# A fused conditioning and attention kernel: division on two engines, first sequences in rows, later weight loads

## The chip, the cores and the metric

The kernel runs on one core of one Trainium2 chip. That core has a tensor engine (PE), a vector engine (DVE), a scalar engine (ACT), GpSimd (POOL) and a sync engine (SP); SP and ACT also issue DMAs. The metric is the device time of one execution in microseconds (us); lower is better. All data are fp32, and weights and inputs start in the chip's memory.

## The reference

There are 32 sequences (B) of 256 tokens (S) with 256 features (D). For each, a cross attention with 16 heads of 16 conditions the input, a transformer of two layers follows (8 heads of 64, a window of 128 tokens with look-back, and a gated feed-forward part with 682 hidden units), and the input is added:

```python
# cond: seq1 = x (keys, values), seq2 = f (queries), seq_len1 = lengths
q = ((seq2 + b_self) @ Wq + bq);  k = (concat([seq1 + b_prev, seq2 + b_self], 1) @ Wk + bk)
v = (concat([seq1, seq2], 1) @ Wv + bv)                  # each split in 16 heads
score_prev = where(arange(l1) < seq_len1, q @ k[:l1].T * SCALE, -inf)
score_self = (q * k[l1:]).sum(-1, keepdims=True) * SCALE   # each query's own token
w = softmax(concat([score_prev, score_self], -1))
cond = (w[..., :-1] @ v[:l1] + w[..., -1:] * v[l1:]) @ Wo + bo
# each of two layers, on h (shift_token: half of the features one token later)
q, k, v = split(shift_token(h) @ wqkv, 3)
q, k = rotary_xpos(l2norm(q) * qs, l2norm(k) * ksc)
h = h + local_attention(q, k, v) @ wo                   # softmax over own and previous window
n = layernorm(shift_token(h)) * lg + lb
a, g = split(n @ w1 + b1, 2);  h = h + (a * gelu(g)) @ w2 + b2
out = x + h
```

## The kernel before

**The planner.** The kernel is not written in the order in which it runs. `tile_kernel` calls methods of `Engine` objects, which only record operations into a `Plan`. PE's operations are recorded in units (`plan.unit`), each with a kind of tiling of the array: full, split in rows (2 or 4) or in columns (2 or 4). `price` gives each operation a cost. `run` then walks the five engines in time by these costs: PE takes the unit with the best `score`, another engine the ready operation with the lowest `rank`. `score` takes the age of a unit (a due time from `PERIOD`, its place, and offsets from the lists `SHIFT`, `FIRST` for the first group and `FINAL` for the last two), a price for another tiling, the backlog that the unit would add to an engine (`STAY`, `ENTER`), and the PSUM banks that it takes (`BANKS`). A full unit marked soft may be cut into column parts when PE is in a column tiling (`parted`). At the end `issue` emits everything in that order, so nearly every instruction of the profile has one line, L567, and is told by its tile's name. A tile written by `either` goes to DVE or ACT, as the planner finds.

**Setup, stage (-1, 0).** `load_sequence(0)` and `load_sequence(1)` load f and x of the first two sequences with `blocks`: four DMAs of 64 KB per tensor on SP, in runs of 128 bytes, so that 32x32 blocks lie as DVE's transpose wants them. ACT's queue carries `wq`, `wk`, `wv`, the biases, `misc` (with the identity and the masks), `wo`, the rope table `rope0`, and in a loop over both layers 15 DMAs each: `wqkv`, the scales, `wout`, `w1`, the norm's vectors, `b1`, `w2`. Each layer has a `b1` unit on PE: its bias plus `w1` applied to the norm's offset `lb`, 40 records of one column and 4 for a packed remainder.

**A group.** There are 16 groups of two sequences (G = 2), in the loop over p:

- `prepared`: DVE transposes f and x into `fT` and `xT` (STREAM_TRANSPOSE). PE projects `cq`, `ck`, `cs` and `vals`; ACT adds biases into `qc` and `kc`. `spread` copies them by 8 DMAs each on SP into `qh` and `kh`, where each head has 16 of 32 rows, and 4 more bring the length mask (`behind`) into `kh`. `self` gives each token's score with itself.
- `conditioned`: four units of scores `S` in row tiling, whose maxima DVE reduces into `mx`; `nm`; a turn `nmT`; `rows` on ACT, and four DMAs of it into `qh`. Then the scores again, transposed (`ST`), exponentials `eT` on ACT, `AV` in column tiling, `oh`, the turn `ohT`, the quotient `at` on POOL, `turn` and the projection `co` into the residual stream `res`.
- `attention`, per layer and sequence: `q`, `k` and `v`; squares `sq` on ACT, their sums `ss`, the rotary products `raw` and `rot` on DVE and POOL; turns `qkT`; scores `sc`; in `weights` the masked maximum, the exponential with its sum `den`, its reciprocal and the division of `ex`; turns `exT`, copied on ACT; `av`; `wout`.
- `feedforward`, per layer for both sequences: the mean, `cen`, `var`, `rstd`, its turn `rs`, `w1` with the gate, `w2`.
- `finished`: DVE turns the result back (`yt`), POOL adds the input, four DMAs store it.

The division of `weights` in this version, four per call, is:

```python
part = (
    es[:, i, 1:3, :].rearrange("p k q -> p q k")
    if w
    else es[:, i, 0, :].rearrange("p (k q) -> p q k", k=2)
)
vec.tensor_scalar(part, part, den[:, i, w : w + 1], None, ALU.mult)
```

The groups overlap: the planner starts `prepared` and `conditioned` of later groups while layers of an earlier one run, and PE always has units of several groups to choose from.

Of the kernel before, what the change touches and what calls it, by code (L numbers as in the profile page):

```python
# [148 lines left out]
class Node:  # L149


    def __init__(self, engine, unit, number):
        self.engine, self.unit, self.number = engine, unit or self, number
        self.ops, self.cost, self.table, self.load = [], 0.0, None, 0.0
        self.after, self.then, self.ready, self.tiles = {}, [], 0.0, set()


class Plan:
# [15 lines left out]
    def __init__(self, tc, engines, pools, make):  # L174
        self.tc, self.engines, self.pools, self.make = tc, engines, pools, make
        self.nodes, self.units, self.unit_, self.group, self.place = [], [], None, 0, 0.0
        self.stage, self.stages, self.done = 0, {}, set()
# [55 lines left out]
    def record(self, engine, name, args, kw):  # L233
# [6 lines left out]
        if engine == "PE":  # L240
            node, wide = u, int(np.prod(out.shape[1:]))
            u.soft = u.soft and name == "matmul" and kw["lhsT"].shape[1] == 128
            cost = (2 if name == "transpose" else 4) * (wide + 2) / 2400 / u.streams
            if name == "transpose" and u.streams > 1:
                cost = max(cost, 0.062 / u.streams)
            cost = max(cost, 0.2) if wide < 64 else cost
            u.small += wide < 64
            turn = 0.65 if name == "transpose" else 1.0 if wide >= 64 else 0.0
            u.weight += cost * turn * self.WORK.get(u.kind, 1.0)
            u.place += cost  # L250
            self.place += cost
        else:
            node = self.node(engine, u)
            self.edge(u, node)
            if name == "dma_start":

                dst, src = kw["out"].shape, kw["in_"].shape
                run = min(dst[-1], src[-1])
                cost, node.load = 0.55, int(np.prod(dst)) / run * max(0.048, run * 4 / 24e3) / 16
            else:  # L260
                cost, node.table = self.price(engine, name, args, kw, size)
                if engine == "X":
                    node.either = {"V": cost, "S": 0.068 + size / 1267}
                u.feeds[engine] = u.feeds.get(engine, 0.0) + cost
# [10 lines left out]
    def price(self, engine, name, args, kw, size):  # L275

        if engine in "VX":
            extra = 0.02 if name == "reciprocal" else 0.0
            if name == "scalar_tensor_tensor":
                extra = 0.06  # L280
            return 0.065 + extra + size / 960, "any" if engine == "X" else None
        if engine == "S":
# [4 lines left out]
            return 0.068 + size / 1267 + extra, table  # L287
        power = any(v is ALU.pow for v in args)
# [5 lines left out]
    def run(self, policy):  # L294
# [6 lines left out]
        self.kind, self.table, pe, blocked = ("full", 1), "any", 0.0, 0.0  # L301
        self.begin()
# [10 lines left out]
        self.idle = self.switches = self.cold = self.wire = 0.0  # L313

# [42 lines left out]
        while todo:  # L357
# [12 lines left out]
            if e != "PE":  # L370
# [3 lines left out]
                cost = n.cost  # L374
                if e == "S" and n.table not in ("any", None, self.table):
                    self.table, cost = n.table, cost + 1.3
# [6 lines left out]
                if n.load:  # L383
                    self.wire = max(self.wire, end) + n.load
                    end = self.wire + self.LANDING
                ended(n, end)
# [151 lines left out]
    def rank(self, n, e):  # L538
        other = e == "S" and n.table not in ("any", None, self.table)
        return n.ready + 2.0 * other, n.number  # L540
# [11 lines left out]
    def issue(self, order):  # L552
# [7 lines left out]
        for n in order:  # L560
# [3 lines left out]
            for name, args, kw in ops:  # L564
                if n.engine in "VS" and name == "copy":
                    name = "tensor_copy" if n.engine == "V" else "copy"
                ins = getattr(self.engines[n.engine], name)(  # L567
# [5 lines left out]
class Engine:  # L573
# [15 lines left out]
    156, 528, 54, -76, 49, 292, -28, 245, 120, -102, -425, 52, -30, 35, 68, 22, 33, 22, -208,  # L589
    -4, 119, -41, 61, 69, 90, 152, 19, 32, -62, -238, 52, -2, 49, -168, 13, -85, -54, -65, 36,  # L590
    64, 112, -439, -349, -167, 223, -408, -5, 62, -46, -234, 56, -27, 119, -7, -45, 96, -17,
    -38, 61, -374, -335, -58, 1, -150, -372, -152, -51, -265, -409, 8, 67, -53, 114, -41, -17,
    -83, 34, 68, 48, 60, -261, -99, -7, -76, -335, -100, -105, -191, -306, -58, 15, -102, 32,
    -23, -66, 39, -309, -188, 106, -258, 33, -30, -139, 22, -141, 82, -290, -255, 32, 19, -99,
    134, 126, 14, -15, -222, -574, -156, 97, 93, -32, -241, 50, 152, -118, -41, -45, 21, -102,
    20, 47, 3, 15, 55, 169, -56, -24, 43, 199, -247, 143, -97, -15, -223, -41, -95, -88, -212,
    -127, -29, -32, -285, -545, -142, -265, -8, -118, -6, 152, 84, -122, 25, 14, 4, 18, 141, 60,
    166, -454, -139, 25, -127, -186, -20,
]
FIRST = [  # L600
    0, 0, 0, 0, 0, 0, 0, 0, 10, 35, -9, 213, 102, 95, 210, -345, -65, -122, -290, 49, -201, 6,
    -193, -61, -7, 106, 99, -6, -100, -16, 106, 13, 65, -266, -137, 7, -58, 247, 58, 69, 48, 1,
    -114, -155, -32, -173, -34, 65, 135, 130, -117, 69, 71, 117, 272, 156, 73, -3, -1, -31, -33,
    -133, 51, 151, 175, 239, 445, 215, 231, 120, 135, 97, -3, -90, -188, -357, -32, -64, -276,
    -297, -374, -330, -535, -346, -72, -135, -217, 156, 27, 182, 40, -174, -48, 77, -252, -118,
    -307, -246, 33, -96, -400, -238, -150, -69, -239, 6, 79, 152, 26, -38, -60, -358, -15, -155,
    89, -99, -69, -60, 87, -3, -114, -222, -118, 60, -143, -246, -29, -171, -319, -115, -49,
    -17, -96, -75, -88, 113, 144, -56, -6, 35, -9, -141, -41, -74, -183, -115, -131, -49, -79,
    109, -65, -145, 55, -88, -244, -157, -153, -264, -181, -118, -121, -82, -23, -37, -86, -83,
    -110, -213, -219, -209, -160, -63, 0, 0,  # L610
]
FINAL = [
    0, 0, 0, 0, 0, 0, 0, 0, 56, -34, 24, 16, 12, 140, -55, -63, -14, 1, -33, -84, -66, -53, -46,
    -145, -40, -121, 67, -19, -32, -29, 98, 97, 8, 45, -119, -130, -61, -106, 67, 94, -33, 8,
    54, 33, 8, -94, -222, -47, -210, -95, -90, -11, -121, 156, 49, 10, 43, 87, 7, 64, -144, -81,
    35, -80, 47, -31, -76, -182, 53, 86, 32, 67, 229, 49, 115, 31, 6, -10, -135, 40, 27, -79,
    -83, -8, 108, -110, 63, -40, -249, -98, -95, -18, -170, -139, -28, -12, -41, 76, 83, 116,
    59, -9, 65, -157, -74, -50, -119, -145, -16, -25, 13, 6, 73, -2, -181, -184, -151, -49, -97,
    116, -8, 56, 187, 15, 69, -31, -42, -59, 109, 161, 193, 112, 209, 211, 117, 80, 41, 59, 77,
    -84, 136, 47, 92, -54, 145, 66, 93, 1, -60, 152, -30, 108, 108, -119, 50, -9, -29, -39, 44,  # L620
    -113, -118, -128, -103, 66, 10, -89, -27, -49, -2, -10, 53, 34, -67, -8,
# [4 lines left out]
def tile_kernel(ctx: ExitStack, tc: tile.TileContext, a: dict, out: bass.AP):  # L626
# [69 lines left out]

    def load_sequence(n, after=()):
        plan.unit(after=after)
        loaded[n] = [blocks(name, src[n]) for name, src in (("ft", f), ("xt", x))]

    load_sequence(0)
    plan.unit()

# [5 lines left out]
    wq, wk, wv = (weight(f"w{n}", a[f"L0_cond_W{n}"], D) for n in "qkv")  # L709
# [10 lines left out]
    bk = column(a["L0_cond_bk"], "bk", 2)  # L720
    bv = kept("bv", (P, D))
    ld(bv, a["L0_cond_bv"].partition_broadcast(P), act)
    ld(misc, a["c_misc"][:, 0:C_IOTA], act)
# [45 lines left out]
    load_sequence(1)  # L769
# [3 lines left out]
    plan.unit()  # L773
    wo = weight("wo", a["L0_cond_Wo"], D)
    bo = column(a["L0_cond_bo"], "bo", 2)
    rope0 = sb2("rope0", P, 2, 4, FD)
    ld(rope0, a["c_rope"].rearrange("(t p) j d -> p t j d", p=P), act)
# [3 lines left out]
    for l in range(DEPTH):  # L781
# [63 lines left out]

    def projected(name, w, j, src):
# [27 lines left out]
    def prepared(n, b):  # L874

        ft, xt = loaded.pop(n)
        plan.unit()
        fT, xT = sb2("fT", P, 2, S), sb2("xT", P, 2, S)
        for dst, src in ((fT, ft), (xT, xt)):
            vec.transpose(dst.rearrange("p c t -> p (c t)"), flat(src))  # L880
# [64 lines left out]
    def conditioned(b, vs, nself, res):  # L945
# [4 lines left out]
        for g in range(4):  # L950
# [12 lines left out]
            for i in range(4):  # L963
                vec.tensor_reduce(mx[:, :, 4 * g + i], sc[i], AX.X, ALU.max)
        nm, es = sm("nm", P, 2, CH), sm("es", P, 2, CH)
# [76 lines left out]
    def attention(l, b, res):  # L1042
# [80 lines left out]
        def weights(c, sc):  # L1123
# [32 lines left out]

            for i in range(2):
                for w in range(2):
                    part = (
                        es[:, i, 1:3, :].rearrange("p k q -> p q k")  # L1160
                        if w
                        else es[:, i, 0, :].rearrange("p (k q) -> p q k", k=2)
                    )
                    vec.tensor_scalar(part, part, den[:, i, w : w + 1], None, ALU.mult)
# [182 lines left out]
    gates = []  # L1347
    for p in range(NG):
# [9 lines left out]
        for b in range(G):  # L1358
            plan.stage = (p, 3 + b)
            done.append(conditioned(b, *heads[b], res))  # L1360
        gates.append(done)
# [16 lines left out]
    AGE, SWITCH, OVER, STAY, ENTER = 0.02, 1.5, 1.0, 6.0, 4.0  # L1378
    HURRY = 0.0
    FEED, MOST, BANKS = 1.0, 3.0, 0.0  # L1380
# [71 lines left out]
```

## Time and profile before

| | |
|---|---|
| Median of 3 runs | 3427.64 us (3423.55 to 3428.22) |
| The profiled execution | 3422.27 us, span 3420.5 us |
| Mean granted clock of PE | 0.99 |
| Busy: PE, DVE, ACT, POOL | 98%, 63%, 52%, 34% of the span |
| First scores `S`, first `ST`, first `q` on PE | 50.6, 85.9, 115.3 us |
| First `rs` (end of the first group's first norm) | 222 us |
| From group to group in the middle | 207.2 us |
| DMA | 69.00 MB; 16 engines 5 tenths busy in the first slice, 0 to 1 later |

The span is the profiled part of one execution; 1.8 us of that execution's time lie around it. A slice is a fortieth of the span, about 85 us. An fp32 matmul shows as two records, a transpose on PE as one. "128*64" in a group's name is the size of the weights that a matmul loads, rows by columns, and "128x1" that of the moving data.

### The profile page before, as it was taken

Reading aid. Unit: us, or ns where it says so; the run is one execution under the profiler, and the core shown is the slowest. Engines: PE = TensorE matmul, PEld = TensorE weight load, DVE = VectorE, ACT = ScalarE, POOL = GpSimd, SP = SyncE. Lnnn points to the kernel's source line nnn. Section 1 sums busy time; section 2 is a strip of 40 time slices with the busy share of each in tenths; the row PEclk is TensorE's granted clock in tenths of the full one; section 3 lists DMA queues with packets and bytes.
Section 4 is the critical chain, followed back from the end, with each engine's and each line's share of the span. In section 5 each row is a group of like instructions: output and inputs, shape, how many; then the busy total and the mean of one; then the engine's idle time right before and its main releaser. Section 6 shows DMA issues by size and latency. Waiting matters only on the chain.

```text
span 3420.5 us, 69279 instructions
## 1 busy us (share of the span) xinstructions
PE 3348.6 (98%) x25984; PEld 1908.7 (56%) x25984; DVE 2161.9 (63%) x6673; ACT 1780.5 (52%) x4537; POOL 1163.4 (34%) x1195
## 2 busy tenths in 40 slices
PE   6999999999999999999999999999999999999998
PEld 5665556465564655656455564655646556465554
DVE  3558567485675747657485674847657486574763
ACT  0556456473554726456373563735547364554653
POOL 0325052250613407043160522507134070432541
PEclk7999999999999999999999999999999999999999
DMA  5100010010101001010010100101010010100001
GB/s 147 20 15 11 12 27 9 16 26 9 26 15 21 17 13 20 16 20 17 13 21 14 27 13 15 24 7 26 16 20 17 13 20 15 27 15 12 4 2 27
DMA packets 310926, 69.00 MB, mean 20 GB/s; under 512 B 286776, under 2 KB 308096, under 8 KB 310592
## 3 DMA queue, kind: packets, MB, share of 16 engines
q1 hardware_dynamic: 298848, 54.24, 9.3%
q10 hardware_dynamic: 11744, 10.34, 1.1%
q8 instruction: 207, 3.39, 0.4%
q14 instruction: 127, 1.04, 0.1%
HBM read 35.53 MB, written 8.39 MB: 13 GB/s over the span
## 4 chain that ended last, share of the span: by engine, by line
PE 77%; DVE 12%; POOL 3%; ACT 1%; issue 1%; POOLq 0%; SPq 0%; DMA 0%; DVEq 0%; ACTq 0%
PE w L567 27%; DVE ex L567 6%; PE wout L567 6%; PE q L567 5%; PE av L567 4%; PE k L567 4%; PE sc L567 4%; PE S L567 4%; PE v L567 3%; PE ST L567 3%; PE vals L567 3%; PE AV L567 3%; PE exT L567 2%; PE qkT L567 2%; DVE rot L567 2%; PE cs L567 2%
## 5 line engine op out<-in xcount | busy, mean ns | idle before, releaser
L567 ACT ACTIVATE ex<-ex,nm,rq 128x128 f32<-128x128 f32 (+1 forms) x1024 | 546.2, 537 | 107.3 <-DVE nm L567 106.1
L567 PE MATMUL w<-cen,w 128*128 128x512 f32 (+2 forms) x1480 | 589.2, 598 | 0.8 <-DVE cen L567 0.3
L567 POOL TENSOR_TENSOR raw<-raw,rot 128x512 f32<-128x512 f32 x256 | 327.6, 1281 | 749.2 <-DVE rot L567 660.3
L567 PEld LDWEIGHTS w<-cen,w 128*128 128x128 f32 (+2 forms) x1480 | 224.9, 175 | 270.7 <-issue 231.4
L567 DVE TENSOR_SCALAR ex<-ex,den 128x128 f32<-128x128 f32 (+1 forms) x1024 | 351.4, 457 | 5.2
L567 DVE TENSOR_REDUCE mx<-S 128x2 f32<-128x512 f32 x512 | 314.3, 686 | 49.4 <-PE S L567 49.3
L567 PE MATMUL w<-act,w 128*128 128x512 f32 (+3 forms) x880 | 324.6, 602 | 2.9 <-DVE act L567 2.8
L567 ACT ACTIVATE eT<-ST 128x512 f32<-128x512 f32 x512 | 263.8, 605 | 115.0 <-PE ST L567 109.8
L567 DVE CUSTOM_DVE_ANT_0 ex<-sc,misc 128x128 f32<-128x128 f32 (+1 forms) x1024 | 299.2, 353 | 31.3 <-PE sc L567 30.8
L567 DVE SCALAR_TENSOR_TENSOR act<-w,b,act 128x512 f32<-128x512 f32 (+1 forms) x192 | 143.4, 748 | 262.0 <-PE w L567 195.5
L567 ACT ACTIVATE act<-w,b 128x512 f32<-128x512 f32 (+1 forms) x192 | 128.9, 686 | 280.1 <-PE w L567 276.8
L567 POOL TENSOR_TENSOR xs<-stream 128x512 f32<-128x512 f32 x32 | 35.0, 1094 | 641.5 <-PE cs L567 318.1
L567 PE MATMUL wout<-qT,wout 128*64 128x256 f32 (+2 forms) x1728 | 242.8, 381 | 0.5 <-DVE nm L567 0.3
L567 PE MATMUL v<-wqkv,stream 128*128 128x512 f32 (+1 forms) x608 | 242.5, 599 | 0.0
L567 PE MATMUL k<-wqkv,stream 128*32 128x512 f32 (+2 forms) x1104 | 239.9, 593 | 0.0
L567 PE MATMUL q<-wqkv,stream 128*32 128x512 f32 (+2 forms) x960 | 237.7, 594 | 0.2 <-ACT stream L567 0.2
L567 ACT COPY exT<-exT 128x384 f32<-128x384 f32 x512 | 207.3, 498 | 54.5 <-PE exT L567 53.8
L567 PEld LDWEIGHTS w<-act,w 128*128 128x128 f32 (+3 forms) x880 | 124.8, 176 | 167.1 <-issue 151.5
L567 POOL TENSOR_TENSOR rq<-ss,minus_half 128x8 f32<-128x8 f32 x128 | 215.1, 1684 | 4.9
L567 POOL TENSOR_TENSOR ss<-ss,minus_half 128x8 f32<-128x8 f32 x128 | 213.3, 1666 | 5.7
L567 PE MATMUL sc<-kT,qT 64*128 64x128 f32 (+1 forms) x2048 | 205.7, 337 | 0.4
L567 PEld LDWEIGHTS wout<-qT,wout 128*64 128x64 f32 (+2 forms) x1728 | 161.6, 147 | 73.0 <-issue 17.6
(127 smaller groups left out, 5520.2 us busy)
## 6 DMA issues: line engine op xcount, KB each, us to landing
ft<-in_fside_BxSxS_dram SPq DMA_DIRECT2D x128, 64.0 KB
xt<-in_x_dram SPq DMA_DIRECT2D x128, 64.0 KB
qh<-qc SPq DMA_DIRECT2D x256, 32.0 KB
kh<-kc SPq DMA_DIRECT2D x256, 32.0 KB
ot<-in_x_dram SPq DMA_DIRECT2D x128, 64.0 KB
out_dram<-ot SPq DMA_DIRECT2D x128, 64.0 KB
wqkv<-in_L_ffn_wqkv_dram ACTq DMA_DIRECT2D x2, 1536.0 KB
w<-in_L_ffn_w_dram ACTq DMA_DIRECT2D x2, 1364.0 KB
```

The lines of the kernel that those rows point to most:

```text
L567: ins = getattr(self.engines[n.engine], name)(*[real(v) for v in args], **{k: real(v) for k, v in kw.items()})
```

## The change

1. The division in `weights` works on contiguous views, `flat[i][w]`, and is recorded as `either.scaled`; `issue` makes of it a `tensor_scalar` on DVE or an activation with a scale on ACT.
2. Sequences 0 and 1 are loaded by `rows`, one DMA of 256 KB per tensor in runs of 1 KB, and turned by PE (`turned_tiles`, as `at` is). The identity is loaded first on ACT's queue, ahead of `wq`; the rest of `misc` follows later, and `wv` after the biases.
3. The loop over the layers becomes `load_layer(l, after)`. It is called in the first group after `conditioned(b)`, for layer b, with the first `S` unit of that sequence as its gate. Each call loads `rope0` again. The gate is an order in the plan.
4. The planner counts with a port that DVE shares with POOL (`port`, `holds`), other prices for `tensor_scalar`, a DMA issue that waits for the eighth DMA before it, and a term `hurry` in `rank`, which is 0. `STAY` goes from 6 to 5, `ENTER` from 4 to 3, `BANKS` from 0 to 1, and all three lists of offsets are new.

```diff
+                inside = [v for v in views if not v.tile.pool == "bank"]
+                two = name in ("scaled", "scalar_tensor_tensor", "tensor_scalar") and size >= 4
+                node.port = engine in "VX" and two and len(inside) == len(views)
+                node.holds = engine == "G" and size >= 64
...
+            if name in ("tensor_scalar", "scaled") and args[0].tile.pool != "bank" and size >= 64:
+                return 0.128 + size / 1920, None
...
+                if n.port and e == "V":
+                    t = max(t, held)
+                elif n.holds:
+                    held = t + cost - 0.12
...
                 if n.load:
-                    self.wire = max(self.wire, end) + n.load
+                    at = max(t, self.landed[-8]) + cost
+                    now[e] = at
+                    self.wire = max(self.wire, at) + n.load
                     end = self.wire + self.LANDING
+                    self.landed.append(end)
...
+                if name == "scaled" and n.engine == "V":
+                    name, args = "tensor_scalar", (*args, None, ALU.mult)
+                elif name == "scaled":
+                    name, args, kw = "activation", (*args[:2], AF.Copy), {"scale": args[2]}
...
+    def rows(name, src):
+        t = sb2(name, P, 2, D)
+        ld(t, src.rearrange("(t p) d -> p t d", p=P))
+        return t
...
-        loaded[n] = [blocks(name, src[n]) for name, src in (("ft", f), ("xt", x))]
+        shape = rows if n < G else blocks
+        loaded[n] = [shape(name, src[n]) for name, src in (("ft", f), ("xt", x))]
 
     load_sequence(0)
     plan.unit()
+    ld(ident, a["c_misc"][:, C_ID : C_ID + P], act)
...
-    for l in range(DEPTH):
+    def load_layer(l, after):
+        plan.unit(after=after)
+        rope0 = sb2("rope0", P, 2, 4, FD)
+        ld(rope0, a["c_rope"].rearrange("(t p) j d -> p t j d", p=P), act)
         wqkv.append(weight(f"wqkv{l}", a["L0_ffn_wqkv"][l], 3 * INNER))
...
-        plan.unit()
-        fT, xT = sb2("fT", P, 2, S), sb2("xT", P, 2, S)
-        for dst, src in ((fT, ft), (xT, xt)):
-            vec.transpose(dst.rearrange("p c t -> p (c t)"), flat(src))
+        if n < G:
+            fT, xT = turned_tiles("fT", ft), turned_tiles("xT", xt)
+            plan.unit()
+        else:
...
...
-                    vec.tensor_scalar(part, part, den[:, i, w : w + 1], None, ALU.mult)
+                    either.scaled(flat[i][w], flat[i][w], den[:, i, w : w + 1])
...
             done.append(conditioned(b, *heads[b], res))
+            if p == 0:
+                plan.stage = (-1, 1 + b)
+                load_layer(b, (begun[4 * b],))
...
-    AGE, SWITCH, OVER, STAY, ENTER = 0.02, 1.5, 1.0, 6.0, 4.0
+    AGE, SWITCH, OVER, STAY, ENTER = 0.02, 1.5, 1.0, 5.0, 3.0
...
-    FEED, MOST, BANKS = 1.0, 3.0, 0.0
+    FEED, MOST, BANKS = 1.0, 3.0, 1.0
```

`begun` collects the `S` units. The lists of offsets, 174 numbers each before and 179 after, are left out.

## The prediction

> **What bounds the kernel now.** I read the page first: span, busy time of the engines, and the 40 slices.
>
> ```profile
> span 3420.5 us, 69279 instructions
> PE 3348.6 (98%) x25984; PEld 1908.7 (56%) x25984; DVE 2161.9 (63%) x6673; ACT 1780.5 (52%) x4537; POOL 1163.4 (34%) x1195
> PE   6999999999999999999999999999999999999998
> PEclk7999999999999999999999999999999999999999
> ```
>
> PE is busy from the second slice to the end. No other engine is above 63%, so the time is what PE's instructions take, plus its rare pauses. The first slice is the exception: 6 tenths busy, at 7 tenths of the clock. The windows view (window; length; PE busy; PEld, DVE, ACT, POOL; clock; DMA share; GB/s) opens it, with 200 us of the middle beside it:
>
> ```profile
> 0.00:10.00 10.00, 2.21 (x11) 2.24 (x11) 2.09 (x7) 0.00 (x0) 0.50 (x5) 1.00 0.79 156
> 10.00:20.00 10.00, 3.04 (x15) 2.95 (x14) 0.49 (x5) 0.00 (x0) 1.89 (x1) 1.00 1.00 249
> 20.00:30.00 10.00, 7.91 (x27) 6.66 (x28) 3.77 (x8) 0.00 (x0) 0.71 (x3) 1.00 0.97 261
> 30.00:40.00 10.00, 7.60 (x40) 6.80 (x38) 4.12 (x20) 2.85 (x5) 0.00 (x0) 0.82 0.78 212
> 40.00:50.00 10.00, 6.06 (x29) 5.97 (x28) 0.27 (x2) 0.00 (x0) 0.00 (x0) 0.50 0.77 230
> 50.00:60.00 10.00, 6.48 (x32) 4.67 (x32) 3.83 (x12) 0.00 (x0) 0.45 (x2) 0.50 0.42 93
> 1700.00:1900.00 200.00, 198.74 (x1589) 112.31 (x1582) 132.06 (x411) 108.10 (x278) 72.21 (x74) 1.00 0.10 18
> ```
>
> For 60 us PE waits for transfers; in the middle it is idle 1.3 us in 200. Next come the rows by form, for operations whose number or shape changes (shape; count; busy us, mean ns; idle before):
>
> ```profile
> L567 DVE TENSOR_SCALAR ex<-ex,den 128x256 f32<-128x256 f32 x512 | 263.8, 518 | 0.0
> L567 DVE TENSOR_SCALAR ex<-ex,den 128x128 f32<-128x128 f32 x512 | 203.0, 396 | 5.2
> L567 PE MATMUL self<-misc,prod 128*128 128x8 f32 x64 | 9.0, 264 | 2.4 <-DVE prod L567 2.4
> L567 PE MATMUL var<-mean_w,sq 128*128 128x1 f32 x48 | 6.0, 246 | 0.0
> L567 PE MATMUL var<-mean_w,sq 128*32 128x1 f32 x96 | 1.3, 172 | 0.0
> ```
>
> A `var` record on the full array takes 6.0/48 = 0.125 us of PE's time, one on 32 columns 0.014. A 1-column record costs nearly the same at any width of weights, and narrow ones lie four side by side, so shape matters. Last, the chain is 77% PE and 12% DVE, and the waits view of 700 to 2900 us gives what PE waited for (total us, times, longest):
>
> ```profile
> PE exT L567 <- ACT sq L567: 5.5, 11, 0.5
> PE ck L567 <- DVE nm L567: 3.4, 11, 1.0
> PE qkT L567 <- DVE rot L567: 2.7, 11, 0.3
> PE turn L567 <- POOL at L567: 2.5, 10, 0.3
> ```
>
> **A price for PE's stream.** The trace's start-to-start times of records that didn't wait are: 0.430 us for 512 columns on the full array, 0.215 in two halves, 0.107 in four quarters (splitting is free for wide ones); 1 column 0.113, 0.026 and 0.010; 8 columns 0.104, 0.029 and 0.009; a 128x128 turn 0.109; and 0.165 extra (0.14 to 0.20) each time PE changes tiling between full, row-split and column-split. Summed in PE's order of before, that gives 3269 us; the 151 us left of the span are lost time: 64 up to the first `rs` at 222 us, 76 in the middle (about 5 a group over 15 groups), 11 in the tail. An fp32 matmul leaves two records, a turn one.
>
> **1. New order on PE: +20 us.** The change carries new SHIFT, FIRST and FINAL lists and planner costs, so every engine's order is new. I counted the compiled order of both kernels. `var` has 68 full matmuls instead of 24, 112 on 64 columns instead of 184, 16 on 32 instead of 48: 2 x (44 x 0.113 - 72 x 0.026 - 32 x 0.010) = +5.6. `self` has 80 instead of 32, 96 instead of 184, none instead of 16: 2 x (48 x 0.104 - 88 x 0.029 - 16 x 0.009) = +4.6. The 16 turns of the first sequences: +1.7. Tiling changes go from 1011 to 1060: 49 x 0.165 = +8.1 (7 to 10). Wide matmuls split less, which is worth nothing. None of this hides behind other work, as PE is the full engine. Bounds +16 to +24; I take +20.
>
> **2. Division: -6 us.** The 1024 `tensor_scalar` on DVE become 672 there and 352 activations on ACT, on contiguous views. Where POOL works, four of them took 2.02 us (at 2148.63), elsewhere 1.14 (at 3343.91):
>
> ```profile
> 2148.63 2.02 DVE L567 TENSOR_SCALAR ex<-ex,den 128x128 f32<-128x128 f32 x4
> 3343.91 1.14 DVE L567 TENSOR_SCALAR ex<-ex,den 128x128 f32<-128x128 f32 x4
> ```
>
> So the strided form already loses time beside POOL, and I give the contiguous form on DVE no gain. DVE's 1024 cover 351 us (the page's row; the two forms above overlap); a third moves: about -115. Against it, 118 more PSUM copies of about 0.42 us move from ACT to DVE: +50; DVE ends near 2100 (61%). ACT gets 352 x 0.37 to 0.48 (its `oh` copy and `qc` activation, 128x256, as bounds) = 130 to 169, 46 more table loads x 1.283 = 59, and loses 118 x 0.38 = 45: about 1940 (57%). Neither becomes the bound. What PE can win is its waits: DVE and ACT's rows above are 11.6 us in 2200, 1.1 a group, and the lost 5 a group holds more in waits too short for that view. Below: a third of the DVE delay gone and half the lost time with it, -38. Above: shorter distances on PE between a producer and its consumer. Counted in stream time at the tightest place, scores to `exT` go from 9.3 to 7.5 us, `k` to `qkT` 8.9 to 7.3, `av` to `wout` 1.7 to 0.5; mean-to-`var` 3.9 to 8.1 and `ohT` to `turn` 4.3 to 8.1 get looser. A distance of 7.5 us has to cover bias and maximum, `nm`, exponential, sums, `den` and division; if the 16 batches a group (256 `den` reciprocals in 16 groups) come 0.13 us late each, +2 a group, +30. The distances moved both ways, so I stay near the waits seen: a third of 1.1 a group over 15 groups, -6.
>
> "ScalarE: Activation LUTs", What ACT_TABLE_LOAD costs, in the Trainium skill adds a drain of about 1380 ns to the 1283 ns of a load and speaks against giving ACT more work. The trace's row has the 1283 ns (96 loads, 123.2 us), but its first load, at 32.41, is followed by `qc` at 33.70, with no room for that drain after it; by the page, the sum for ACT would be 63 us higher, 59% of the span, and still no bound.
>
> **3. Start: -4 us.** Now `cq` waits until 22.1 us for `fT`; four 64 KB DMAs in 128-byte runs per tensor and 27 DMAs on ACT's queue share the transfers (DMA share 1.00 in 10 to 20 us). `qc` waits on ACT behind those 27, until 33.70. `S` waits for the copies `kc` to `kh` until 50.6 and 58.1; `ST` starts at 85.9. After: one 256 KB DMA per tensor, 12 fewer on SP, 16 turns and four 128x512 copies (0.69 us each on DVE); all 16 turns stand first on PE, so all four tensors must be there: with `wq`, `wk` and the identity 1.6 MB, 6.5 us at the 250 GB/s of 10 to 20 us, 2.5 of landing, 0.7 of issue, about 4 for turns at half clock and a copy: projections start near 14. Their 14 units and 14 us of stream at mixed clock, with ACT beside them, put `qc` and `kc` near 29.5. The weights get no semaphore on the scores: what holds them back is ACT's program order, so they start near 30, with one rope load of 256 KB more. Each DMA here waits for the one eight before it over both queues (landings 2.2 to 2.5 us alone, 9.2 behind `wqkv`), so SP's 40 copies to `qh` and `kh` stand in the same line as the weights. Queued behind that: `S` (52 and 57 to 60 us), and on ACT the `rows` activations, since ACT issues a layer's loads in 23 to 25 us (33.7 to 58.4 in before) and is free near 74. The two layers' `b1` sums, once at 36.5 to 46 at half clock and 69.2 to 74.2 warm, now both stand ahead of `ST`: 10 us warm, 19 cold. `ST` comes at 79 to 91. PE has 41.8 us of stream behind it there instead of 38.1, so the gain is 85.9 - (79 to 91) + 3.7 = -1.4 to 10.6. Middle: 4.
>
> "TensorE: Matmul & The Clock Gate", What's actually happening, says that about 3.4 us of sustained work releases the full clock. The windows agree in direction (0.50 at 40 to 60, 0.81 and 0.70 at 60 to 80); by the page, both `b1` sums would run warm if the work ahead of them has no gap, which is the 79 end.
>
> **4. Tail: 0.** PE's last operations are equivalent; 11 us are lost there now, plus or minus 1.
>
> **Sum.** The profiled execution took 3422.3 (span 3420.5), 5.4 below the median of 3427.64. 3422.3 + 20 - 6 - 4 = 3432.3, or 3437.7 as a median; I say 3437.
>
> **Rivals.** A measurement can tell 0.2% (6.9 us), so "same" is 3420.8 to 3434.5.
> Faster (0.36): DVE's delays in the division, not PE's order, make the 5 us lost a group. With half of them gone (-38) and the best start (-10.6): 3422.3 + 20 - 38 - 11 = 3393, as a median 3399; with 2 of 5, 3414. It decides from 3437.7 + 6 - 3420.8 = 23 us, or 1.5 us a group. For: four divisions at 2.02 instead of 1.14. Against: only 1.1 a group is seen in waits.
> Tie (0.13): 0.6 to 1.4 us a group less: about 3428.
> Much slower (0.14): the tight chains come late by 1 us a group or more: 3437.7 + 6 + 15 = 3459.
> The new loading does nothing (inside the forecast): the weights are on PE's path in neither kernel, DMA order eats the gain: 3441.
> The forecast case has 0.37, with its own range 3434 to 3447. Faster 0.36, same 0.13, slower 0.51. The range goes from half of the faster case to the much slower one: 3402 to 3460.
>
> **What the profile would show.** Right: about 1060 tiling changes, `var` 128*128 x136 near 17 us, `self` x160 near 22; POOL-time divisions still near 2 us for four; ST at 79 to 91; 200-us windows in the middle with PE idle as now, and a longer period per group (207.2 to 208). Wrong: if a group takes under 206 us, the stalls were the larger term; if `ST` starts before 75 or after 95, the queue was misread; if ACT or DVE shows over 70%, the division was.

## The result: 1.3% slower, and the profile after

The changed kernel takes 3469.8 us (median of 4, 3469.0 to 3470.3) against 3427.0 for the kernel before beside it: ratio 1.0132, interval 1.0120 to 1.0144 (the two medians alone give 1.0125). The direction that had the larger chance came true, but the size is four times the forecast's +10 us, and above the top of the range.

The page of the profiled execution (3469.9 us):

```profile
span 3468.1 us, 66932 instructions
PE 3389.0 (98%) x24964; PEld 1967.3 (57%) x24964; DVE 2097.2 (60%) x6436; ACT 1923.0 (55%) x4820; POOL 1163.2 (34%) x1195
...
PE   7999999999999999999999999999999999999997
PEclk7999999999999999999999999999999999999999
```

PE is again the only full engine, DVE and ACT stand where they were forecast, and 47.6 us more have passed, 40.4 of them as busy time of PE. So busy shares say nothing here; the sum has to be split by stage. I priced PE's compiled order with the same start-to-start times as in the prediction ("stream") and took the difference to the trace as lost time:

| stretch (us) | before | after | longer by | of it stream | of it lost |
|---|---|---|---|---|---|
| start to the first `rs` | 222.0 | 227.6 | 5.6 | 4.4 | 1.2 |
| first `rs` of group 0 to that of group 15 | 3117.4 | 3150.1 | 32.7 | 16.7 | 16.0 |
| from there to PE's last record | 69.6 | 78.7 | 9.1 | -0.2 | 9.3 |
| PE's last record to the end | 11.5 | 11.7 | 0.2 | | |

A steady group (the fourth to the twelfth) takes 210.8 us instead of 207.3: stream 204.4 instead of 203.0, lost 6.4 instead of 4.3.

The table compares two single executions. That of before is 4.7 us under its median, that of after is at its own, so 47.6 us stand here for the 42.8 between the medians. The start alone can vary by this much: b_flat below, with before's order, has its first `rs` at 227.2 instead of 222.0.

Lost time holds at least two things: pauses of PE, and stretches in which the granted clock is 0.50 and the same stream takes longer. From start to the first `rs` PE is idle 23.0 us instead of 29.4, and the clock is at half for 68.3 us instead of 54.6; in the middle (the table's second row) it is 38.1 idle instead of 31.0, and 30.7 at half instead of 6.8; behind that, to PE's last record, 6.2 idle instead of 0.0, and 6.8 at half instead of 0.0. If half clock costs half of its time (an estimate), this makes 0.5, 19.1 and 9.6 us more, where the last column has 1.2, 16.0 and 9.3 more.

Where the middle loses shows in the waits view of 700 to 2900 us (total us, times, longest), three lines where before had several small ones:

```profile
PE exT L591 <- ACT exT L591: 10.4, 11, 0.9
PE exT L591 <- ACT sq L591: 10.3, 11, 0.9
PE exT L591 <- DVE rot L591: 8.4, 11, 0.8
```

All 29.1 us are `exT`, the turns that need the divided weights. Two of the three lines come from one place in every group, in the timeline (start, length, instruction, and in brackets the idle time before it; DVE, PE and ACT lines in turn):

```profile
1580.23 1.03 DVE L591 TENSOR_SCALAR ex<-ex,den 128x128 f32<-128x128 f32 x4
1582.30 1.39 PE L591 MATMUL exT<-misc,ex 64*128 64x64 f32 x36
1584.46 0.24 PE L591 MATMUL exT<-misc,ex 64*128 64x64 f32 x1 [0.77 <-DVE rot L591]
1585.65 0.65 PE L591 MATMUL exT<-misc,ex 64*128 64x64 f32 x11 [0.94 <-ACT exT L591]
1583.26 0.60 ACT L591 ACTIVATE sq<-k 128x512 f32<-128x512 f32 x1 [0.20 <-DVE rot L591]
1583.75 1.48 ACT L591 ACTIVATE ex<-ex,den 128x128 f32<-128x128 f32 x4
1585.14 3.12 ACT L591 COPY exT<-exT 128x384 f32<-128x384 f32 x8
```

PE starts its turns at 1582.30 and has to stop at 1583.7: four divisions sit on ACT behind a square, end at 1585.2, and the copies that empty PE's banks come only after them. The waits view names other operations, which ended later than the divisions that stand between; that the divisions count is read here from the order on ACT, and a_tiny below tests it. The third line, on `sq`, is a second place 41 us earlier: PE stops from 1542.5 to 1543.4, and ACT runs five divisions from 1541.10 on, then a square, then the copies.

The pauses are not all. Right behind the place above the granted clock falls (windows view: start:end, length, PE, PEld, DVE, ACT, POOL busy, clock, DMA share, GB/s):

```profile
1582.60:1586.00 3.40, 1.69 (x45) 1.44 (x43) 2.74 (x7) 3.19 (x9) 1.61 (x3) 1.00 0.00 0
1586.00:1589.40 3.40, 3.40 (x27) 2.56 (x25) 3.40 (x13) 2.25 (x6) 3.40 (x4) 0.50 0.00 0
```

From 700 to 2900 us this place comes eleven times, and eight times the clock falls behind it, for 3.4 us each; it falls nowhere else there, and in before not once. Groups with such a fall take 211.1 us, those without it 209.5, though their pauses are the same; why three places have none is not shown.

The start, in the windows view:

```profile
20.00:30.00 10.00, 10.00 (x48) 8.79 (x48) 3.23 (x9) 2.00 (x6) 0.00 (x0) 1.00 0.14 28
30.00:40.00 10.00, 5.91 (x36) 5.32 (x34) 2.38 (x7) 0.42 (x1) 0.00 (x0) 0.82 0.73 260
40.00:50.00 10.00, 0.00 (x0) 0.00 (x0) 0.00 (x0) 0.00 (x0) 0.00 (x0) 0.50 0.70 221
70.00:80.00 10.00, 10.00 (x48) 8.53 (x48) 6.15 (x11) 0.64 (x3) 0.65 (x3) 0.50 0.65 187
80.00:90.00 10.00, 10.00 (x49) 9.93 (x49) 1.66 (x14) 0.37 (x1) 0.00 (x0) 0.50 0.01 3
90.00:100.00 10.00, 10.00 (x77) 7.50 (x77) 0.69 (x3) 4.03 (x8) 0.00 (x0) 0.50 0.00 0
```

The first 30 us are what the change means to do: PE is full from 10 us on. Then it stands for 16.1 us for a copy `qh<-qc`, and the clock stays at half until 100 us, through both `b1` sums (8.69 and 8.53 us for 40 records each). `cq` starts at 14.2, `S` at 52.0, `ST` at 92.9.

And the tail: a 20-us window of before, 40 us ahead of its end, and the same place of after:

```profile
3360.50:3380.50 20.00, 20.00 (x135) 8.82 (x132) 7.12 (x12) 1.81 (x3) 3.38 (x3) 1.00 0.09 14
```

```profile
3408.00:3428.00 20.00, 15.02 (x89) 6.82 (x86) 9.03 (x17) 1.23 (x2) 5.83 (x5) 0.86 0.14 21
```

PE is idle 5 us there, between the last group's `mean`, `var`, `rs` and `w1`, and the clock is 0.86 instead of 1.00. Before, 32 records of `w2` units lay in these gaps; now 12 do, and the others have been spent earlier.

The counted shapes are there too, as forecast (17 and 22 us):

```profile
L591 PE MATMUL self<-misc,prod 128*128 128x8 f32 x160 | 20.6, 256 | 0.0
L591 PE MATMUL var<-mean_w,sq 128*128 128x1 f32 x136 | 16.6, 243 | 0.3 <-DVE mx L591 0.3
```

### The profile page after: what moved, and what is told of

It is laid out like the page before. It is cut to its first block, busy times and chain, and to the rows that moved or that the text cites. A ratio compares the mean times of both kernels' runs of the same rounds, so it can differ in the third digit from the quotient of the medians.

```text
span 3468.1 us, 66932 instructions
## 1 busy us (share of the span) xinstructions
PE 3389.0 (98%) x24964; PEld 1967.3 (57%) x24964; DVE 2097.2 (60%) x6436; ACT 1923.0 (55%) x4820; POOL 1163.2 (34%) x1195
## 4 chain that ended last, share of the span: by engine, by line
PE 84%; DVE 7%; ACT 6%; DMA 1%; POOL 1%; issue 1%; SPq 0%; POOLq 0%; ACTq 0%; DVEq 0%
PE w L591 27%; PE wout L591 6%; PE av L591 5%; PE q L591 5%; PE sc L591 4%; PE ST L591 4%; PE S L591 4%; PE v L591 4%; PE k L591 4%; PE AV L591 4%; ACT ex L591 4%; PE vals L591 3%; PE exT L591 2%; DVE ex L591 2%; PE cq L591 2%; PE qkT L591 2%
## 5 line engine op out<-in xcount | busy, mean ns | idle before, releaser
L591 PE MATMUL v<-wqkv,stream 128*128 128x512 f32 (+2 forms) x540 | 247.5, 606 | 0.0
L591 PE MATMUL k<-wqkv,stream 128*128 128x512 f32 (+2 forms) x848 | 242.7, 594 | 0.2 <-ACT v L591 0.2
L591 PE MATMUL q<-wqkv,stream 128*128 128x512 f32 (+2 forms) x808 | 240.6, 597 | 1.3
L591 DVE TENSOR_SCALAR ex<-ex,den 128x128 f32<-128x128 f32 (+1 forms) x672 | 207.3, 368 | 4.9
```

The source lines that it names most:

```text
L591: ins = getattr(self.engines[n.engine], name)(*[real(v) for v in args], **{k: real(v) for k, v in kw.items()})
```

## The experiments

Times are medians, ratios are to the kernel before, run beside it on the same chip (its medians there: 3421 to 3424 us). "Own order" means that the planner's finished order of all engines was kept and only the stated edit made to it.

### The division, with the order held

**b_flat**: before, contiguous views.

```diff
-                    vec.tensor_scalar(part, part, den[:, i, w : w + 1], None, ALU.mult)
+                    vec.tensor_scalar(flat[i][w], flat[i][w], den[:, i, w : w + 1], None, ALU.mult)
```

> The kernel before in its own order, the 1024 divisions still on DVE but on contiguous views. Theory (the contiguous form is worth nothing by itself): 3427 within 5 us, DVE ex rows as before. Rival (the contiguous form is held longer while POOL works): slower by 10 us or more, four divisions beside POOL above 2.3 us. Second rival (it is cheaper and frees DVE): faster by 7 us or more.

Measured: 3419.3, ratio 0.9986 (0.9977 to 0.9995). By form:

```profile
L567 DVE TENSOR_SCALAR ex<-ex,den 128x256 f32<-128x256 f32 x512 | 199.3, 389 | 0.0
L567 DVE TENSOR_SCALAR ex<-ex,den 128x128 f32<-128x128 f32 x512 | 175.8, 343 | 4.9
```

389 and 343 ns instead of 518 and 396: the contiguous form is cheaper, and that is worth some 4 us (lost time in the middle 72.1 instead of 76.1). It lies between the first expectation and the third.

**b_third**: the same, and 11 of every 32 divisions done by ACT at their place in the order.

```diff
+            if n.engine == "V" and ops and ops[0][0] == "divided":
+                count += 1
+                n.engine = "S" if count % 32 < 11 else "V"
```

> The kernel before in its own order, contiguous divisions, 352 of 1024 done by ACT at the same place of the order. Theory (a division on ACT stands behind exponentials, squares and copies that ACT runs in order, and ahead of the exT copies, so PE's exT turns wait for it): slower, 3435 to 3460, with waits of exT on ACT in the middle. Rival (only the new order of PE made the kernel slower, an ACT share relieves DVE): 3420 to 3430.

Measured: 3515.8, ratio 1.0266 (1.0250 to 1.0281); a group takes 214.1 us instead of 207.0.

```profile
PE exT L575 <- ACT sq L575: 39.1, 11, 3.6
PE exT L575 <- ACT ex L575: 6.0, 10, 0.6
```

Before has 5.5 us in the first of these lines and none in the second. PE's order is the same to the instruction, so this is the move of the division to ACT alone: far more than I expected, but at the expected place. In the middle PE is idle 80.8 us instead of 26.3 in b_flat, and the clock is at half for 88.7 us instead of 10.2, so the falls of the clock behind the pauses are a large part of the price.

**a_dve**: after, every division on DVE at its place in after's order.

```diff
-                if name == "scaled" and n.engine == "V":
+                engine = n.engine
+                if name == "scaled":
+                    name, args, engine = "tensor_scalar", (*args, None, ALU.mult), "V"
```

> The changed kernel in its own order, but every division is done by DVE at its place in that order. Theory (about 2 us a group of PE's new waits are divisions on ACT): the middle loses 4 to 5 us a group instead of 6.4, so 3440 to 3455. Rival (the waits come from shorter distances in PE's order, wherever the division is done): 3465 to 3480, since DVE now has more to do at the same places.

Measured: 3519.1, ratio 1.0274 (1.0259 to 1.0290); 214.2 us a group. Neither expectation holds: it is slower by far more than either said. The waits of `exT` come to 38 us in 700 to 2900 (16.7 on `sq`, 11.2 on `exT`, 10.3 on DVE's `ex`). An order planned for one split of the division is late with the other split, in both directions. By itself this run tells against ACT as the cause; the next one decides.

**a_tiny**: after, the 352 divisions on ACT on 8 columns only. It leaves the other columns undivided; the order of all engines is after's.

```diff
-                    name, args, kw = "activation", (*args[:2], AF.Copy), {"scale": args[2]}
+                    part = args[1][:, 0:8]
+                    name, args, kw = "activation", (part, part, AF.Copy), {"scale": args[2]}
```

> The changed kernel in its own order; the 352 divisions on ACT work on the first 8 columns only, so most of that third of the weights stays undivided. Theory (ACT's time for these divisions ahead of the exT copies makes the new waits of exT): waits of exT in 700 to 2900 us fall from 29 to below 12 us, the middle to 208 to 209.5 a group, time 3440 to 3455. Rival (the order's short distances alone): waits and period as now, 3462 to 3470.

Measured: 3439.2, ratio 1.0048 (1.0032 to 1.0063): 30 us off the changed kernel, as the theory said. A group takes 208.4 us, and

```profile
PE exT L592 <- ACT exT L592: 3.6, 11, 0.3
PE exT L592 <- ACT ex L592: 3.3, 11, 0.8
PE exT L592 <- ACT sq L592: 2.2, 10, 0.2
```

9.1 us of `exT` waits instead of 29.1. Lost time per group falls to 3.9, below before's 4.3; what is left, 1.1 us a group more than before, is after's stream of 204.4. So ACT's time for its third of the divisions (155 us, of which this saves 77) makes the new stalls, and the counted stream is a cost of its own. The 30.4 us that the middle gets shorter are 18.3 us less idle time of PE (19.8 instead of 38.1) and a clock that never falls there (0.0 us at half instead of 30.7).

### The order

**b_lists**: before with after's three lists, unit by unit.

```diff
-            u.shift = SHIFT[number]
...
+            u.shift = TABLE[cls][",".join(str(x) for x in key[1:])]
```

> The kernel before with its own planner, division and loading, and only the three lists of offsets taken from the changed kernel, unit by unit. Its counted PE stream is 3305 us, 36 above before. Theory (the order is fitted to everything that the planner sees, and the new lists in another program give a poor one; stalls come on top): 3460 to 3500. Rival (the lists are as good, and the other parts of the change made it slower): 3420 to 3440.

Measured: 3572.4, ratio 1.0440 (1.0424 to 1.0456); 216.2 us a group, of it stream 205.7 and lost 10.5.

**a_plan_dve**: after, whose planner puts every division on DVE and finds its own order.

```diff
-                    either.scaled(flat[i][w], flat[i][w], den[:, i, w : w + 1])
+                    vec.scaled(flat[i][w], flat[i][w], den[:, i, w : w + 1])
```

> The changed kernel, whose planner is told that every division is on DVE and makes its own order. Its counted PE stream is 3296 us, 27 above before and 6 above the changed kernel. Theory (the order's fit decides, the engine of the division does not): 3460 to 3500. Rival (the ACT share of the division is what made it slower): 3425 to 3445.

Measured: 3623.7, ratio 1.0589 (1.0571 to 1.0608); 218.3 us a group, lost 13.7, with PE waiting for `wout<-ACT qT` (17.2 us) and `S<-DVE cen` (15.8). Both times lie beyond the upper end of what I expected. The lists belong to one program: take them elsewhere, or change one thing that the planner sees, and the order is some 150 us worse than the one it came from (3572.4 against 3421.4, and 3623.7 against 3469.8). The clock has its part in this too: in the middle it is at half for 92.4 and 183.9 us. So a division of the 43 us among planner, lists and program can't be had by exchanging them one by one.

### The start

**a_late**: after's own order; the layers' weights issued by SP behind the last `kc` copy, one rope load, the layers' small work and `b1` sums behind the first and fourth `ST`.

```diff
+    for n in loads:
+        n.engine = "D"
+    last = max(k for k, n in enumerate(order) if n.mark == "spread")
+    order = order[: last + 1] + memsets + loads + order[last + 1 :]
```

> The changed kernel in its own order, but the two layers' weights are issued by SP behind the last kc to kh copy instead of by ACT, the rope table is loaded once, and the layers' small preparations and b1 sums stand behind the first and the fourth ST unit. Theory (the weights, placed by ACT's program order in front of the copies, cost the start about 25 us): first S near 38, first ST at 62 to 70, time 3440 to 3452. Rival (what follows ST is limited by ACT's exponentials and the start has no more to give): first ST earlier, but less than 8 us won, 3462 to 3470.

Measured: 3476.7, ratio 1.0155 (1.0136 to 1.0174), outside both expectations. `S` came at 40.2, `ST` at 82.3 only, with one wait:

```profile
PE ST L594 <- DMA qh<-rows: 18.4, 1, 18.4
```

The copies of `rows` now stood behind the weights on SP. The wait had moved, not gone.

**a_late2**: the weights behind those copies, the `b1` sums behind the fourth and eighth `ST`.

```diff
-    last = max(k for k, n in enumerate(order) if n.mark == "spread")
+    last = max(k for k, n in enumerate(order) if n.mark == "nm_row")
```

> The changed kernel in its own order, with the layers' weights issued by SP behind the copies of rows into qh (not only behind those of kc), the rope table loaded once, and the layers' preparations and b1 sums behind the fourth and the eighth ST unit. Theory (in the run with weights behind the kc copies the queue only moved the wait, to ST on qh<-rows, 18.4 us): S near 40, ST at 62 to 70, first q 15 to 25 us earlier than 122.7, time 3445 to 3458. Rival (after ST, ACT's exponentials or the weights' own landing hold q at 115 or later): ST early, but 3462 to 3472.

Measured: 3464.4, ratio 1.0123 (1.0108 to 1.0138). `ST` at 64.2 as expected, but the first `b1` sum waited 9.3 us for its own transfer in front of `AV`, and `q` started at 120.8; the time is the rival's.

**a_late3**: both `b1` sums ahead of the first `mean`.

```diff
+        at = means[0] - 30
+        order = order[:at] + copies + order[at:]
+        order = place_bank(order, at + len(copies), unit, adds, 6)
```

> As the run before with the weights behind the copies of rows (ST at 64, but the first b1 sum waited 9.3 us for its transfer and stood ahead of the next AV), now with both b1 sums and what follows them moved ahead of the first mean of the first group. Theory (PE's order of the b1 sums holds the start): first q at 95 to 105 instead of 120.8, first rs near 208 instead of 225.6, time 3444 to 3454. Rival (ACT's exponentials hold the start): first q at 112 or later, 3458 or more.

Measured: 3460.4, ratio 1.0110 (1.0086 to 1.0134). `q` started at 92.7, 30 us earlier than in after, yet the first `rs` came at 217.5 instead of 227.6: the gain was a third of that, and the time is the rival's. The windows show where the rest went:

```profile
170.00:180.00 10.00, 9.63 (x126) 7.35 (x122) 2.89 (x15) 7.68 (x18) 0.00 (x0) 0.95 0.01 3
180.00:190.00 10.00, 10.00 (x49) 10.00 (x48) 0.23 (x2) 0.00 (x0) 0.00 (x0) 0.50 0.00 0
190.00:200.00 10.00, 10.00 (x109) 6.64 (x108) 1.77 (x5) 0.00 (x0) 0.00 (x0) 0.70 0.01 2
```

The sums stood at 176 to 192.6 with no gap, after full work at full clock, and the clock fell to half during them: 16.4 us instead of 10. I had taken their cost as that of a warm stretch; but it fell while nothing but they ran.

**b_rows**: b_flat, and the first two sequences by one DMA each, turned on PE, the identity first; weights as in before.

```diff
+            n.ops = [("dma_start", (), dict(out=whole, in_=src.rearrange("(t p) d -> p t d", p=P)))]
...
+        u.ops = [
+            ("transpose", (pt[:, c, t * P : (t + 1) * P], tile_src[:, t, c * P : (c + 1) * P], ident), {})
+            for c in range(2)
+            for t in range(2)
+        ]
```

> The kernel before in its own order, contiguous divisions on DVE (3419 as measured), and in addition the first two sequences loaded by one DMA each, turned on PE, and the identity loaded first; the layers' weights stay where they were. Theory (qc waits for ACT's 27 DMA issues, not for the data): projections start 6 to 8 us earlier, S within 3 us of 50.6, time 3414 to 3423. Rival (the loading itself is the gain of the start): S at 44 or earlier, 3405 to 3414.

Measured: 3410.0, ratio 0.9962 (0.9946 to 0.9977): by its time the rival. `S` at 44.4 instead of 50.8, `ST` at 80.2, first `rs` at 211.5 instead of 227.2 in b_flat. This beats both kernels. (The two profiled executions, 3406.9 and 3423.5, lie further apart than the medians; by these the gain over b_flat is 9.3 us.)

**b_rows_b1**: b_rows with both `b1` sums ahead of the first `mean`.

```diff
+        order = [n for n in order if n is not unit and n not in adds and n not in copies]
+        at = next(k for k, n in enumerate(order) if n.engine == "PE" and first_out(n) == "mean") - 30
```

> As the run with the kernel before, contiguous divisions and the first sequences in rows (3410), with both b1 sums moved ahead of the first mean. Theory (the first b1 sum takes 9.7 us at half clock ahead of S, and costs half of that in a warm stretch): S 5 to 9 us earlier than 44.4, time 3400 to 3406. Rival (S waits for the kc to kh copies anyway): S at 43 or later, 3406 to 3412.

Measured: 3425.5, ratio 1.0006 (0.9995 to 1.0017), 15 us worse than b_rows. Both expectations miss. `S` did come at 41.1, but PE was idle more in 30 to 60 us, and the clock was low for longer. Windows of b_rows, then of this run:

```profile
90.00:100.00 10.00, 8.06 (x77) 4.45 (x76) 2.95 (x10) 4.61 (x11) 2.70 (x5) 1.00 0.19 31
100.00:110.00 10.00, 10.00 (x100) 4.42 (x100) 3.38 (x8) 5.43 (x12) 1.50 (x2) 1.00 0.17 28
```

```profile
90.00:100.00 10.00, 8.24 (x59) 3.98 (x62) 2.31 (x8) 2.71 (x7) 2.30 (x4) 0.67 0.18 29
100.00:110.00 10.00, 10.00 (x60) 5.90 (x56) 0.42 (x1) 4.96 (x10) 0.00 (x0) 0.53 0.17 28
```

The first `rs` came at 233.2 instead of 211.5. Up to there PE was idle 23.0 us instead of 15.8, and the clock was at half for 78.5 us instead of 44.4, so both have a part in these 22 us, the clock the larger by this count. The sums themselves did get cheaper, 12.9 us together instead of 14.4. Why the clock stays low longer is not shown; and the two profiled executions are the fastest of b_rows and nearly the slowest of this run (3406.9 and 3429.7 for medians of 3410.0 and 3425.5).

### The tail

**a_tail**: after's own order, two `w2` units of group 14 put around the last `var`, and that group's turning back and stores behind the last `rs`.

```diff
+    order = order[:var] + [second, order[var], tail] + order[var + 1 :]
+    order = order[: rstd + 1] + adds + yt + order[rstd + 1 :]
+    order = order[: hl + 1] + ots + stores + order[hl + 1 :]
```

> The changed kernel in its own order but for its end: two of the w2 units of the last group but one stand just ahead of and just behind the last var instead of ahead of the last exT, and that group's transposes back, its additions on POOL and its stores follow the last rstd and rs. Theory (the tail lost 9 us because nothing covers the chain from the last mean over var and rs to w1): waits of var on sq and of rs on rstd shrink from 4.1 to under 2 us together, the stretch from the last group's first rs to the end from 78.7 to 72 to 76, time 3462 to 3467. Rival (the chain is as long with cover, or av and wout wait instead): 77 or more, time 3468 to 3474.

Measured: 3466.4, ratio 1.0127 (1.0110 to 1.0144). The stretch from the last group's first `rs` to PE's last record takes 76.3 us instead of 78.7; the waits of `var` and `rs` shrink from 4.1 to 0.3, but `w1` now waits 2.6 for `cen`, behind the transposes that I had put on DVE there. A quarter of the 9 us came back: the gaps are the mechanism, though this edit doesn't close them all.

## Why the prediction was wrong, step by step

- **What bounds the kernel** held: PE is full, and the ledger of its stream and its lost time carries the whole difference (4.4 + 16.7 - 0.2 = 20.9 us of stream, 1.2 + 16.0 + 9.3 = 26.5 lost).
- **Step 1, the new order, +20**: held. The stream by the same prices is +21, and the forms of `var` and `self` have the predicted counts; that is the same count once more and no test of the prices. The test is a_tiny: its middle has 11.2 us less idle time than before's and 6.8 us less at half clock, and yet is 2.3 us longer (3119.7 against 3117.4), so its stream must be some 17 us longer.
- **Step 2, the division, -6: this step failed.** Measured is +16 in the middle, in pauses of PE and in the clock that falls behind them; no term of my sum stood for the clock there. I reasoned by load ("neither becomes the bound") and by the length of waits seen before. Both were beside the point: DVE ended at 60%, ACT at 55%, as forecast. What decides is ACT's program order. A division on ACT stands in line behind squares and exponentials and ahead of the `exT` copies, and PE's `exT` needs both. My sentence on distances that get shorter (scores to `exT` 9.3 to 7.5 us, with an upper bound of +30) named the right place; then I chose the value near the small waits of before. b_third (+7.1 us a group in an unchanged PE order) shows this, with a split that no planner had seen; a_tiny (-2.4 a group in after's own order) sizes it. I also gave the contiguous form on DVE no gain; it has one, 389 instead of 518 ns and about 4 us of time, so the term was mis-sized there too.
- **Step 3, the start, -4**: the chain was read well (`cq` 14.2 for 14, `kc` done at 30.4 for 29.5, weights from 30, `S` 52.0 for 52, ACT free at 76.1 for 74), and its end was not: `ST` at 92.9 lies behind the 91 of the range, and lost time to the first `rs` grew by 1.2. Both `b1` sums ran at half clock. The start as a whole came out 5.6 us longer where I had 4 us shorter, and a part of that is the spread of 5 us that before's order shows by itself. The new loading of the sequences is a gain (b_rows, about 9 us over b_flat); in the changed kernel PE is idle 6.4 us less up to the first `rs`, but 13.7 us more at half clock. a_late to a_late3 show the place of the weights and of the sums costing 30 us at the first `q`, but only 10 at the first `rs`.
- **Step 4, the tail, 0: failed.** I compared PE's last operations as a list, and they are equivalent; I didn't look at what stood between `mean`, `var` and `rs`. The lost time grew by 9.3 there.
- **The rivals**: "much slower" had the right mechanism (tight chains come late, at least 1 us a group; 2.1 were measured) and a chance of only 0.14. The faster rival needed DVE's delay to be the lost time; after relieved DVE and lost more. It also counted on 38 of the 76 us lost in the middle of before, of which the trace shows 31.0 as idle time and 6.8 at half clock; what the rest is stays open.
- **The signs of being wrong**: none of the three came (a group under 206 us, `ST` outside 75 to 95, ACT or DVE over 70%). None of them looked for a group much longer than 208, which is what came. Two of the signs of being right stayed out (`ST` at 79 to 91, a group of 207.2 to 208).
- **The rules weighed**: the Trainium skill, "TensorE: Matmul & The Clock Gate", What's actually happening, says that some 3.4 us of sustained work bring the full clock, and by it I allowed the sums to run warm if the work ahead of them had no gap. a_late3 gives the counter-example: 16 us of PE without a gap, and the granted clock falls from 0.95 to 0.50 meanwhile. So the measurement decides: sustained one-column matmuls did not hold the full clock here.

What stays open: whether other lists for the changed program would remove its 16 us of lost time; a search over them wasn't tried. Nor were the planner's own changes (the port, the prices, `STAY`, `ENTER`, `BANKS`) tested one by one.

## What to carry to other kernels

Moving work to an engine with room costs whatever it delays in that engine's queue: ask what stands ahead of it and which producer's next work stands behind it, not how busy the engine is. When a scheduler writes the order, count the new order's stream, and look at each short chain where the other engine's queue has just become longer; small waits before did not tell of the waits after. Read the granted clock of the middle, too: here each pair of pauses in one place could cost as much again through it. A transfer moved off one queue is in front of something on the next, so follow it to the first consumer that is late, and keep the cheap part (here the rows and the contiguous views, 3410 us) when the bundle loses.

## What the runs showed of the hardware

- One-column matmuls let the clock drop though PE shows no gap: 80 such records in 16.4 us, PE busy 10.00 of 10, clock 0.50 (a_late3, 180 to 190 us). In after the same sums took 8.69 and 8.53 us for 40 records, warm 4.52 before. In b_flat, b_rows_b1, a_late and a_late2 one sum starts at full clock, and 2.4 to 4.1 us later the time from record to record goes from 112 to 213 ns.
- Two pauses of 0.8 and 0.9 us in a full stream were followed by 3.4 us at half clock in eight of the eleven places from 700 to 2900 us of after (in one of them PE busy 1.69 of 3.40 us, then clock 0.50). In a_tiny, with pauses of some 0.3 us at ten of these places, the clock didn't fall.
- The clock of the start differs between executions of one order: at 60 to 70 us 0.81 in before and 0.50 in b_flat, which has before's order; first `rs` at 222.0 and 227.2.
- A division as a contiguous `tensor_scalar` takes 389 ns where the strided view of the same 128x256 took 518, means over the whole run. On ACT the same division takes 500 ns, and 295 ns for 8 columns: more than half of its cost there does not go with the width.
